# Two layers of a graph network on one core: a second dense row beside the input stage, list steps in the stage of x

## The chip, the cores and the metric

One core of a Trainium2 chip. The metric is the device time of one launch in microseconds (us), all in 32-bit floats.

## The reference

x is (8, 2048, 128), adj (2048, 2048) with about 0.4% of its entries set and a full diagonal. Two layers, each followed by a residual and a layer norm:

```python
# layer 0, on x, with R = adj
res = si[:, :, None] + sj[:, None, :] + R * w_r + g_b      # si, sj: x @ two columns of g_w
y = (res @ x) @ weight + bias
x = layernorm(x + y)
# layer 1, A1 = A2 = adj
x1 = A.T @ x ;  x2 = 2 * A.T @ x1 - x
y = relu(stack(x, x1, x2, x1, x2) @ Theta1 + bias)
x = layernorm(x + y)
```

Layer 0's sums over si, sj and g_b have rank 9 over the batch, so what remains of it is one product of the sparse R with x @ weight. Layer 1 is two products with the transposed adj ("hops").

## The kernel before, in words

The 2048 nodes are 16 blocks of 128. `Y` holds x @ weight for all 16 blocks on chip (each block 128 x 1024, 8 batches by 128). Rows 0 to 3 of R's blocks are kept transposed and dense in `at4`; their products with Y are whole ("dense rows", `full_rows`). For the rows of blocks 4 to 15, the kernel finds out which rows of each strip of columns have entries, makes lists of them, and multiplies only gathered rows.

Every instruction is tied to program order on its engine (`Tied`, line 67), so the order written is the order run on each queue. All lines are therefore recorded at L72, and groups are read by their tiles.

Stages, in order:

- **Stage of R** (loop over `R_ORDER`, line 328). Step k loads a row of blocks of adj into one of three buffers (`rc`), TensorE transposes its 16 blocks four at a time into a bank, and ScalarE copies them out, scaled, to `at4`, `rct` or `Y` (`row_groups`, line 244). `transposes` (line 237) takes banks in turn from `turns`: 6, 7, 4, 5. VectorE reduces row and column masks (lines 252 to 262). Some steps (`x_at`, line 189) also take a block of x: 8 transposes (`x_t`), then `y_of` (line 277) multiplies by `wx` into banks 2 and 3 by turns, and ScalarE copies to Y. There are NX = 10 such x blocks in this stage, and after each but the first one product of dense row 0 is accumulated in banks 0 and 1. Transposed rows of blocks 4 to 11 are stored to `rr_d` at once.
- **`pump`** (line 216) issues SP's loads and stores from the list `todo`, in its order: the rows of adj three ahead, the blocks of x six ahead, then stores of rows 12 to 15 ("s"), then copies of adj into `rr_d` ("c").
- **Stage of x** (line 666): the remaining six x blocks, each with one product of row 0. Between them: `ranked` at n = 11, `candidates` and the eight rounds of the first lists at n = 13 (VectorE: `max` and `match_replace`). Then Y is stored to `y0_d`.
- **Lists and dense rows** (lines 756 to 825): `lists_end(0)` gives the first indices; from then on GpSimd gathers. A **job** is the gathers of one list of one block: "T" four gathers, "H" three. `get_job` issues them, and `keep_job` has VectorE copy what landed into `rc` and `rct`; four jobs are in flight over four buffers (`st`), and those of blocks 0 to 3 use one buffer (`trp`). `next_job` is a keep and a get. Of the 32 jobs, 20 are fetched here. Around them TensorE does dense row 1 (banks 2, 3), `column_sums` (banks 4, 5, set to zero ahead of the stage of x), `make_ub`, dense rows 2 and 3, `make_u` of finished blocks (through banks 4, 5) and VectorE the rounds of the second lists (`rounds2`), `z_add` and `layernorm`. `lists_end(1)` (line 469) ends the second lists and the test `over`, which decides on a dense fallback at the end that isn't taken.
- **Loop over blocks 4 to 15** (line 828): `get_rows` gathers rows of `y0_d` into twelve buffers in Y (G, line 689), seven gathers a block; `own_rows`, `rank9`, `listed` multiply; `z_add`, `make_u`, `layernorm` follow. Eight jobs are fetched in it (blocks 4 to 7, 9, 11, 13, 15).
- **Two hops** (line 860), 16 blocks each with seven gathers a block; the first fetches the last four jobs.

Of the kernel before, what the change touches and what calls it, by code (L numbers as in the profile page):

```python
# [18 lines left out]
def kernel(  # L19
# [37 lines left out]
    W = 3 * P  # L57
    T_ORDER = list(range(6, NC)) + [4, 5]
    NP = LR + NC - LT
    R_ORDER = [0, 4, 5, 6, 1, 7, 8, 9, 2, 10, 11, 12, 3, 13, 14, 15]  # L60
    NX = 10
    X_ORDER = list(range(ND, NC)) + list(range(ND))
    X_SLOT = [0, 1, 3, 4, 2, 5]
    assert D == P and B == 8 and NC == 16
# [37 lines left out]
    def by4(t):  # L102
        return t.rearrange("p (b f) -> p b f", b=4)
# [79 lines left out]
    ats += [Y[:, n:n + 2].rearrange("p c b f -> p (c b f)") for n in X_ORDER[NX::2]]  # L183

    def at_of(c):
        t = at4[:, c] if c < ND else ats[(c - ND) % 5]
        return t.rearrange("p (j i) -> p j i", i=P)

    def x_at(k):
# [86 lines left out]

    def y_of(n, xt):
        for b in range(0, B, 2):
            py = bank[2 + b // 2 % 2][:, 0:2 * (D + 2)].rearrange("p (i f) -> p i f", i=2)
            for i in range(2):  # L280
                pe.matmul(py[:, i, :], xt[b // HB][:, (b + i) % HB, :], wx, start=True, stop=True)
            act.copy(Y[:, X_ORDER[n], b:b + 2, :], py[:, :, 0:D])
            act.copy(sraw[:, X_ORDER[n], b:b + 2, :], py[:, :, D:D + 2])
# [22 lines left out]
                )  # L306

    LAST = list(range(ND)) + list(range(8, NC)) + list(range(4, 8))
    js_first = [X_ORDER[0]] + [LAST[0]] * (ND - 1)

    def full_rows(c, accs, js):
        at = at_of(c)
# [33 lines left out]
    dve.tensor_add(th[:, 4, :], th[:, 2, :], th[:, 4, :])  # L346
    dve.tensor_sub(th[:, 2, :], th[:, 0, :], th[:, 4, :])
    dve.tensor_add(th[:, 0, :], th[:, 4, :], th[:, 4, :])
    dve.tensor_add(th[:, 1, :], th[:, 1, :], th[:, 3, :])

# [58 lines left out]
    dve.tensor_reduce(miss[:, 1:2], both, AX.XY, ALU.add)  # L409
    for b in bank[4:6]:  # L410
        dve.memset(b, 0.0)

    def encode2():
        dve.tensor_sub(NS_[:, 0:LT, :], NS_[:, 0:LT, :], et)
# [54 lines left out]
    def lists_end(part):  # L469
        b = bank[6 + part]  # L470
        if part == 0:
            lo, hi = 0, NT
            for r in range(2):
                pe.matmul(
                    b[64 * r:64 * r + 64, 0:NT], lists, ident[:, 64 * r:64 * r + 64], start=True,
                    stop=True, skip_group_check=True, tile_position=(0, 64 * r),
                )
        else:
            lo, hi = NT, NI
            for r in range(2):  # L480
# [12 lines left out]
        dve.scalar_tensor_tensor(rown, rown, float(NC), col[:, s], op0=ALU.mult, op1=ALU.add)  # L493
        dve.tensor_copy(idr[:, s], rown)
        if part:
            dve.tensor_reduce(miss[:, 2:3], has, AX.X, ALU.add)
            dve.tensor_sub(miss[:, 0:1], miss[:, 0:1], miss[:, 1:2])
            dve.tensor_sub(miss[:, 0:1], miss[:, 0:1], miss[:, 2:3])
            pe.matmul(
                b[0:1, 64:65], miss[:, 0:1], ones[:, 0:1], start=True, stop=True,  # L500
                skip_group_check=True,
            )
            dve.tensor_scalar(over, b[0:1, 64:65], 0.5, None, op0=ALU.is_gt)

    adj128 = adj.rearrange("n (c f) -> (n c) f", f=P)

# [135 lines left out]
    for k in range(4):  # L642
        x1t.append(rct[:, k * BD:(k + 1) * BD].rearrange("p (b f) -> p b f", b=B))

    def make_u(c, z, xt, u):
        for h in range(2):
            b = transposes([z[:, h * HB + i, :] for i in range(4)])
            act.copy(xt[:, h * HB:(h + 1) * HB, :], b)
        for h in range(2):
            b = by4(bank[4 + h])  # L650
# [11 lines left out]
        get_job()  # L662


    turns[:] = [6, 7]
    for n in range(NX, NC):
        xt = x_t(n)
        pump()
        y_of(n, xt)
        if n == 13:  # L670
            candidates()
            for r in range(8):
                round_of(lists, cand, r)
        full_rows(0, acc0, [X_ORDER[n - 1]])
        if n in (NX, NX + 1, 13):
            s_rows(X_ORDER[4 * max(0, n - NX - (n == 13))])
        if n == 11:
            ranked()
    s_rows(0)
    full_rows(0, acc0, [X_ORDER[NC - 1]])  # L680
    pump()
    assert not todo

# [69 lines left out]
        load_own(0, y0_d, c, Y[:, c] if c < 8 else ring[:, c % 2], c < 8)  # L753


    acc1 = acc_pair()
    full_rows(1, acc1, LAST[0:4])
    lists_end(0)
    get_job()
    get_job()  # L760
    encode2()
    get_job()
    get_job()
    for c0 in range(0, NC, 4):
        column_sums(c0)
    full_rows(1, acc1, LAST[4:5])
    split2()
    make_ub()
    load_z(ND + 1)
    candidates2()  # L770
    full_rows(1, acc1, LAST[5:8])
    next_job()
    rounds2([0])
    next_job()
    si_t(0)
    rank9(0, acc0)
    rounds2([1, 2])
    next_job()
    z_add(acc0, zs[0])
    rounds2([3, 4])  # L780
    next_job()
    rounds2([5, 6])
    next_job()
    rounds2([7])
    full_rows(1, acc1, LAST[8:])
    si_t(1)
    rank9(1, acc1)
    lists_end(1)
    z_add(acc1, zs[1])
    next_job()  # L790
    layernorm(zs[0], "0_0")

    acc2 = acc_pair()
    full_rows(2, acc2, LAST[:8])
    make_u(0, zs[0], x1t[0], u_of[0])
    next_job()
    layernorm(zs[1], "0_1")
    next_job()
    full_rows(2, acc2, LAST[8:])
    si_t(2)  # L800
    rank9(2, acc2)
    for _ in range(2):
        next_job()
    z_add(acc2, zs[2])
    make_u(1, zs[1], x1t[1], u_of[1])
    next_job()
    layernorm(zs[2], "0_2")

    acc3 = acc_pair()
    full_rows(3, acc3, LAST[:8])  # L810
    for _ in range(3):
        next_job()
    own0(ND)
    own0(ND + 1)
    full_rows(3, acc3, LAST[8:])
    for _ in range(2):
        next_job()
    get_rows(0, ND, "T", y0_d)
    get_rows(0, ND, "H", y0_d)
    get_rows(0, ND + 1, "T", y0_d)  # L820
    si_t(3)
    rank9(3, acc3)
# [5 lines left out]
    for c in range(ND, NC):  # L828
        if c > ND:
            if c > ND + 1:  # L830
                get_rows(0, c, "T", y0_d)
            get_rows(0, c, "H", y0_d)
        if c < 10:
            keep_job()
            if c < 8:
                get_job()
            else:
                keep_job()
        elif c % 2:
            keep_job()  # L840
# [12 lines left out]
        for n in [c - 2] if c < 14 else [12, 13] if c == 14 else [14]:  # L853
            make_u(n, zs[n], x1t[n], u_of[n])
        if c + 2 < NC:
            load_z(c + 2)
        layernorm(zs[c], f"0_{c}")


    def hop(i, src, order, there, between):  # L860
# [51 lines left out]
        for k, c in enumerate(order):  # L912
# [117 lines left out]
```

## Time and profile before

| | |
|---|---|
| median of 3 runs | 816.0 us (814.28 to 816.8) |
| the profiled execution | 811.46 us |
| its span | 809.7 us |
| TensorE, VectorE, ScalarE, GpSimd busy | 720.0, 394.8, 188.7, 443.3 us |

| stage, by the trace | us | TensorE busy | transfer engines busy |
|---|---|---|---|
| R | 16 to 105 | 76.3 of 89 | 1.07 |
| x | 105 to 140 | 31.4 of 35 | 1.07 |
| lists and dense rows | 140 to 260 | 111.3 of 120 | 0.66 |
| loop over blocks 4 to 15 | 260 to 428 | 152.2 of 168 | 0.93 |
| first hop | 428 to 629 | 180.9 of 201 | 0.93 |
| second hop | 629 to 810 | 163.5 of 181 | 0.89 |

In a line of the trace the first number is the start in us, the second the length, then the engine, the operation, out<-in by tiles, the shape and the count of records merged. A matmul of 32-bit floats leaves two records. In brackets stands how long the engine idled just before, and what released it. TensorE's busy time counts the pipeline's tail, so it overstates the work done.

### The profile page before, as it was taken

The page shows a single profiled execution, that of the slowest core. Times are in us where ns is not written, and L with a number is a line of the kernel's source. Part 1 is how long each engine was busy: PE and PEld are TensorE (multiplying, and loading weights), DVE is VectorE, ACT ScalarE, POOL GpSimd, SP SyncE. Part 2 cuts the span into 40 slices and gives each one's busy share as a digit, 9 for nine tenths or more (in the row PEclk, how much of TensorE's full clock was granted, in tenths as well). Part 3 has the DMA queues.
Part 4 walks back from the last instruction along what each step waited for, and adds up shares of the span by engine and source line. Part 5 has one row for each costly group of instructions (what it writes and reads, how often), then busy time and mean ns, then how long its engine had stood idle before and what let it go on. Part 6 is the DMA issues. An engine that isn't in the chain of part 4 may idle for free.

```text
span 809.7 us, 10066 instructions
## 1 busy us (share of the span) xinstructions
PE 720.0 (89%) x3554; PEld 365.2 (45%) x3554; DVE 394.8 (49%) x591; ACT 188.7 (23%) x439; POOL 443.3 (55%) x432
## 2 busy tenths in 40 slices
PE   4987989996999989897998788989999899999992
PEld 4766756442543334444354233433444345544441
DVE  5776586587342555655442000000000377777775
ACT  3775755101120223323232000000000011111111
POOL 1000000477677777767635677776664777787650
PEclk8998999997999999999899899999999999999996
DMA  7999999996343999999988799899999799999982
GB/s 264 340 349 352 342 311 309 321 414 215 105 148 92 306 341 351 382 377 342 328 302 315 245 347 369 308 372 392 351 362 345 259 353 357 371 386 374 378 300 70
DMA packets 165300, 253.91 MB, mean 314 GB/s; under 512 B 17255, under 2 KB 118020, under 8 KB 163192
## 3 DMA queue, kind: packets, MB, share of 16 engines
q0 software_dynamic: 49280, 146.52, 49.8%
q1 hardware_dynamic: 93200, 81.01, 30.9%
q10 hardware_dynamic: 22760, 25.63, 8.9%
q8 instruction: 30, 0.49, 0.3%
q14 instruction: 30, 0.25, 0.1%
HBM read 234.82 MB, written 58.72 MB: 363 GB/s over the span
## 4 chain that ended last, share of the span: by engine, by line
PE 48%; DMA 34%; issue 7%; ACT 4%; DVE 3%; POOL 2%; ACTq 0%; SPq 0%; POOLq 0%; DVEq 0%
PE bank L72 48%; DMA Y<-u_d,idx 14%; DMA Y<-y_d,idx 7%; DMA st<-rr_d,idx 4%; DMA ring<-in_x_dram 3%; DMA rd<-rr_d 2%; DMA rc<-in_adj_dram 1%; ACT Y L72 1%; DMA trp<-in_adj_dram,idr 1%; POOL Y L72 1%; DVE st L72 1%; ACT rct L72 1%; ACT trp L72 1%; POOL st L72 1%; ACT at L72 1%
## 5 line engine op out<-in xcount | busy, mean ns | idle before, releaser
L72 POOL DMA_INDIRECT Y<-y_d,idx x196 | 215.4, 1099 | 87.9 <-PE bank L72 39.0
L72 PE MATMUL bank<-Y,rc 128*32 128x512 f32 (+2 forms) x896 | 218.7, 609 | 22.2 <-DMA Y<-u_d,idx 19.8
L72 POOL DMA_INDIRECT st<-rr_d,idx x84 | 86.2, 1026 | 176.2 <-DVE rown L72 146.9
L72 POOL DMA_INDIRECT Y<-u_d,idx x112 | 110.9, 990 | 61.7 <-PE bank L72 25.8
L72 PEld LDWEIGHTS bank<-Y,rc 128*32 128x32 f32 (+2 forms) x896 | 58.9, 128 | 178.9 <-issue 89.9
L72 PE MATMUL bank<-Y,at 128*128 128x512 f32 x256 | 115.9, 603 | 0.0
L72 PE MATMUL bank<-Y,rct 128*32 128x512 f32 (+2 forms) x336 | 75.8, 643 | 9.0 <-DMA Y<-y_d,idx 9.0
L72 DVE TENSOR_REDUCE s<-sq 128x4 f32<-128x512 f32 x64 | 43.9, 686 | 64.4 <-ACT sq L72 64.4
L72 PEld LDWEIGHTS bank<-Y,at 128*128 128x128 f32 x256 | 47.8, 193 | 54.4 <-issue 54.3
L72 DVE COPY ring<-bank 128x512 f32<-128x512 f32 x10 | 6.9, 692 | 115.5 <-PE bank L72 115.5
L72 ACT ACTIVATE sq<-ring 128x512 f32<-128x512 f32 x44 | 27.7, 630 | 122.4 <-DVE ring L72 81.0
L72 PE MATMUL bank<-ring,rd 128*128 128x512 f32 x108 | 51.7, 601 | 3.2 <-DVE ring L72 2.5
L72 DVE TENSOR_REDUCE st<-rc 128x64 f32<-128x2048 f32 x16 | 36.5, 2283 | 32.3 <-DMA rc<-in_adj_dram 32.3
L72 PE MATMUL bank<-ident,rc 128*128 128x128 f32 (+2 forms) x302 | 40.1, 292 | 12.4 <-DMA rc<-in_adj_dram 12.4
L72 PE MATMUL bank<-th,at 128*128 128x128 f32 x384 | 47.6, 277 | 1.9 <-ACT at L72 1.9
L72 ACT COPY ring<-bank 128x512 f32<-128x512 f32 x34 | 19.9, 585 | 121.6 <-PE bank L72 121.6
L72 PEld LDWEIGHTS bank<-th,at 128*128 128x128 f32 x384 | 45.2, 192 | 6.7 <-ACT at L72 3.8
L72 PEld LDWEIGHTS bank<-Y,rct 128*32 128x32 f32 (+2 forms) x336 | 20.4, 133 | 56.5 <-issue 36.3
L72 PEld LDWEIGHTS bank<-ident,rc 128*128 128x128 f32 (+2 forms) x302 | 35.9, 153 | 18.4 <-issue 13.7
L72 PE MATMUL bank<-wx,trp 128*128 128x130 f32 x256 | 36.4, 285 | 8.4 <-ACT sraw L72 6.1
L72 DVE TENSOR_TENSOR ring<-bank,ring 128x512 f32<-128x512 f32 x26 | 17.5, 687 | 52.8 <-PE bank L72 46.3
L72 PE MATMUL bank<-ident,ring 128*128 128x128 f32 x232 | 32.2, 284 | 7.1 <-DMA ring<-in_x_dram 5.6
(142 smaller groups left out, 788.6 us busy)
## 6 DMA issues: line engine op xcount, KB each, us to landing
rc<-in_adj_dram SPq DMA_DIRECT2D x16, 1024.0 KB, 9.8
ring<-in_x_dram SPq DMA_DIRECT2D x25, 512.0 KB, 10.4
rr_d<-in_adj_dram SPq DMA_DIRECT2D x12, 1024.0 KB, 11.1
y_d<-Y SPq DMA_DIRECT2D x16, 512.0 KB, 10.8
rr_d<-rct SPq DMA_DIRECT2D x6, 1024.0 KB, 9.4
rr_d<-Y SPq DMA_DIRECT2D x6, 1024.0 KB, 11.7
u_d<-ring ACTq DMA_DIRECT2D x12, 512.0 KB, 7.2
ring<-y_d SPq DMA_DIRECT2D x11, 512.0 KB, 15.8
```

The lines of the kernel that those rows point to most:

```text
L72: return lambda *a, **k: tc.keep_in_program_order(f(*a, **k))
```

## The change

NX is 8 instead of 10, so two x blocks move from the stage of R to the stage of x. Rows 0 and 1 of R are loaded first, and each x block after the first is followed by a product of row 0 and one of row 1, in banks 0 to 3. To make room, `y_of` moves to banks 4 and 5, and the transposes of R have banks 6 and 7 alone. `ats` has six buffers instead of five. The list steps are called from within the stage of x; the zeroing of banks 4 and 5 moves behind the first round of the second lists. After the stage of x, the column sums and both ranks follow at once; row 2 uses banks 4 and 5, row 3 banks 2 and 3, and the first two `make_u` banks 0 and 1. The test `over` moves to `overflow`, after row 2. 16 jobs are fetched before the loop, ten in it (blocks 4 to 12 and 14) and six in the first hop.

```diff
-    R_ORDER = [0, 4, 5, 6, 1, 7, 8, 9, 2, 10, 11, 12, 3, 13, 14, 15]
-    NX = 10
+    R_ORDER = [0, 1, 4, 5, 6, 2, 7, 8, 9, 10, 3, 11, 12, 13, 14, 15]
+    NX = 8
...
-    todo += [("x", 10), ("x", 11), ("s", 12), ("s", 13), ("x", 12), ("x", 13), ("s", 14), ("s", 15)]
-    todo += [("x", 14), ("x", 15)] + [("c", c) for c in T_ORDER]
+    todo += [("x", 8), ("s", 12), ("x", 9), ("s", 13), ("x", 10), ("x", 11), ("s", 14), ("x", 12)]
+    todo += [("s", 15), ("x", 13), ("x", 14), ("x", 15)] + [("c", c) for c in T_ORDER]
...
-    turns = [6, 7, 4, 5]
+    turns = [6, 7]
...
-            py = bank[2 + b // 2 % 2][:, 0:2 * (D + 2)].rearrange("p (i f) -> p i f", i=2)
+            py = bank[4 + b // 2 % 2][:, 0:2 * (D + 2)].rearrange("p (i f) -> p i f", i=2)
...
-    acc0 = acc_pair()
+    acc0, acc1 = acc_pair(), acc_pair()
...
                 full_rows(0, acc0, [X_ORDER[m - 1]])
+                full_rows(1, acc1, [X_ORDER[m - 1]])
...
+    def lists_at(n):
+        if n == 9:
+            ranked()
+        if n == 10:
+            candidates()
+            for r in range(8):
+                round_of(lists, cand, r)
+            dve.tensor_reduce(miss[:, 1:2], both, AX.XY, ALU.add)
+            thetas()
+        if n == 13:
+            lists_end(0)
+            get_job()
+            get_job()
+            encode2()
+            get_job()
+            get_job()
+        if n == 14:
+            split2()
+        if n == 15:
+            candidates2()
+
     for n in range(NX, NC):
         xt = x_t(n)
         pump()
         y_of(n, xt)
...
+        lists_at(n)
+        for c, acc in enumerate((acc0, acc1)):
+            full_rows(c, acc, [X_ORDER[n - 1]])
...
+    rounds2([0])
+    for b in bank[4:6]:
+        dve.memset(b, 0.0)
+    next_job()
+    rounds2([1, 2])
+    next_job()
     for c0 in range(0, NC, 4):
         column_sums(c0)
...
     make_ub()
     load_z(ND + 1)
...
+    rounds2([3, 4])
     next_job()
     si_t(0)
+    si_t(1)
     rank9(0, acc0)
+    rank9(1, acc1)
+    rounds2([5, 6])
+    next_job()
+    rounds2([7])
+    lists_end(1)
     z_add(acc0, zs[0])
...
     z_add(acc1, zs[1])
     next_job()
     layernorm(zs[0], "0_0")
...
+    acc2 = bank[4:6]
+    full_rows(2, acc2, LAST[:5])
+    next_job()
+    next_job()
+    make_u(0, zs[0], x1t[0], u_of[0], 0)
     layernorm(zs[1], "0_1")
...
+    full_rows(2, acc2, LAST[5:11])
+    next_job()
+    make_u(1, zs[1], x1t[1], u_of[1], 0)
+    next_job()
+    full_rows(2, acc2, LAST[11:])
     si_t(2)
     rank9(2, acc2)
...
     z_add(acc2, zs[2])
+    overflow()
     next_job()
     layernorm(zs[2], "0_2")
...
+    acc3 = bank[2:4]
     full_rows(3, acc3, LAST[:8])
...
+    next_job()
+    next_job()
+    get_rows(0, ND, "T", y0_d)
+    get_rows(0, ND, "H", y0_d)
     own0(ND)
     own0(ND + 1)
     full_rows(3, acc3, LAST[8:])
...
+    keep_job()
+    keep_job()
     get_rows(0, ND + 1, "T", y0_d)
...
-        if c < 10:
+        if c < 15:
             keep_job()
...
-        if c > 8 and c % 2:
+        if c < 13 or c == 14:
             get_job()
...
-            if i == 1 and k % 2 and k < 10:
+            if i == 1 and (k % 2 and k < 12 or k == 12):
                 keep_job()
-                if k < 9:
+                if k < 12:
                     get_job()
```

More of the change, by code (lines that the diff above doesn't have):

```diff
@@ L185, in at_of @@
     def at_of(c):
-        t = at4[:, c] if c < ND else ats[(c - ND) % 5]
+        t = at4[:, c] if c < ND else ats[(c - ND) % len(ats)]
         return t.rearrange("p (j i) -> p j i", i=P)
@@ L308 @@
     LAST = list(range(ND)) + list(range(8, NC)) + list(range(4, 8))
-    js_first = [X_ORDER[0]] + [LAST[0]] * (ND - 1)
+    js_first = [X_ORDER[0]] * 2 + [LAST[0]] * (ND - 2)
     def full_rows(c, accs, js):
@@ L344, with thetas @@
     mask_columns(NC - 1)
[L346 to L349, printed above, removed]
+    def thetas():
+        dve.tensor_add(th[:, 4, :], th[:, 2, :], th[:, 4, :])
+        dve.tensor_sub(th[:, 2, :], th[:, 0, :], th[:, 4, :])
+        dve.tensor_add(th[:, 0, :], th[:, 4, :], th[:, 4, :])
+        dve.tensor_add(th[:, 1, :], th[:, 1, :], th[:, 3, :])
     e2 = rc[:, 4608:4608 + 2 * NP * HC].rearrange("p (q l) -> p q l", l=2 * HC)
@@ L408 @@
     dve.tensor_reduce(miss[:, 0:1], hs, AX.XY, ALU.add)
-    dve.tensor_reduce(miss[:, 1:2], both, AX.XY, ALU.add)
-    for b in bank[4:6]:
-        dve.memset(b, 0.0)
     def encode2():
@@ L498, in lists_end, with overflow @@
             dve.tensor_sub(miss[:, 0:1], miss[:, 0:1], miss[:, 2:3])
[L499 to L503, printed above, removed]
+    def overflow():
+        b = bank[turns[turn[0] % len(turns)]]
+        turn[0] += 1
+        pe.matmul(
+            b[0:1, 0:1], miss[:, 0:1], ones[:, 0:1], start=True, stop=True, skip_group_check=True,
+        )
+        dve.tensor_scalar(over, b[0:1, 0:1], 0.5, None, op0=ALU.is_gt)
     adj128 = adj.rearrange("n (c f) -> (n c) f", f=P)
@@ L643, with make_u @@
         x1t.append(rct[:, k * BD:(k + 1) * BD].rearrange("p (b f) -> p b f", b=B))
-    def make_u(c, z, xt, u):
+    def make_u(c, z, xt, u, o=4):
         for h in range(2):
@@ L649, in make_u @@
         for h in range(2):
-            b = by4(bank[4 + h])
+            b = by4(bank[o + h])
             for i in range(HB):
@@ L662, in next_job @@
         get_job()
-    turns[:] = [6, 7]
+    def lists_at(n):
[18 more added lines that the diff above has]
+            candidates2()
     for n in range(NX, NC):
@@ L669 @@
         y_of(n, xt)
[L670 to L678, printed above, removed]
+        lists_at(n)
+        for c, acc in enumerate((acc0, acc1)):
+            full_rows(c, acc, [X_ORDER[n - 1]])
+        if n % 4 == 0:
+            s_rows(X_ORDER[n - 4])
+        if n == 9:
+            s_rows(X_ORDER[0])
     s_rows(0)
-    full_rows(0, acc0, [X_ORDER[NC - 1]])
+    for c, acc in enumerate((acc0, acc1)):
+        full_rows(c, acc, [X_ORDER[NC - 1]])
     pump()
@@ L753, in own0 @@
         load_own(0, y0_d, c, Y[:, c] if c < 8 else ring[:, c % 2], c < 8)
[L756 to L763, printed above, removed]
+    rounds2([0])
[4 more added lines that the diff above has]
+    next_job()
     for c0 in range(0, NC, 4):
         column_sums(c0)
-    full_rows(1, acc1, LAST[4:5])
-    split2()
     make_ub()
     load_z(ND + 1)
[L770 to L773, printed above, removed]
+    rounds2([3, 4])
     next_job()
     si_t(0)
+    si_t(1)
     rank9(0, acc0)
[L777 to L781, printed above, removed]
+    rank9(1, acc1)
     rounds2([5, 6])
@@ L784 @@
     rounds2([7])
-    full_rows(1, acc1, LAST[8:])
-    si_t(1)
-    rank9(1, acc1)
     lists_end(1)
+    z_add(acc0, zs[0])
     z_add(acc1, zs[1])
@@ L791 @@
     layernorm(zs[0], "0_0")
-    acc2 = acc_pair()
-    full_rows(2, acc2, LAST[:8])
-    make_u(0, zs[0], x1t[0], u_of[0])
+    acc2 = bank[4:6]
+    full_rows(2, acc2, LAST[:5])
     next_job()
+    next_job()
+    make_u(0, zs[0], x1t[0], u_of[0], 0)
     layernorm(zs[1], "0_1")
+    full_rows(2, acc2, LAST[5:11])
     next_job()
-    full_rows(2, acc2, LAST[8:])
+    make_u(1, zs[1], x1t[1], u_of[1], 0)
+    next_job()
+    full_rows(2, acc2, LAST[11:])
     si_t(2)
     rank9(2, acc2)
-    for _ in range(2):
-        next_job()
     z_add(acc2, zs[2])
-    make_u(1, zs[1], x1t[1], u_of[1])
+    overflow()
     next_job()
     layernorm(zs[2], "0_2")
-    acc3 = acc_pair()
+    acc3 = bank[2:4]
     full_rows(3, acc3, LAST[:8])
-    for _ in range(3):
-        next_job()
+    next_job()
+    next_job()
+    get_rows(0, ND, "T", y0_d)
+    get_rows(0, ND, "H", y0_d)
     own0(ND)
@@ L815 @@
     full_rows(3, acc3, LAST[8:])
[L816 to L819, printed above, removed]
+    keep_job()
+    keep_job()
     get_rows(0, ND + 1, "T", y0_d)
@@ L832 @@
             get_rows(0, c, "H", y0_d)
-        if c < 10:
+        if c < 15:
             keep_job()
[L835 to L840, printed above, removed]
-        if c > 8 and c % 2:
+        if c < 13 or c == 14:
             get_job()
```

## The prediction

> **What bounds the kernel now.** I read the page's slices first, then TensorE's timeline, then GpSimd's, then the chain of waits.
>
> ```profile
> PE   4987989996999989897998788989999899999992
> ```
>
> ```profile
> POOL 1000000477677777767635677776664777787650
> DMA  7999999996343999999988799899999799999982
> ```
>
> A slice is 20.2 us. TensorE is near full nearly everywhere. The transfer engines are full up to 190 us and from 270 us on, but a third busy in between (slices 11 to 13). GpSimd, idle until 150 us, is then steadily busy. So no one engine bounds the whole; the bound changes by stage.
>
> Stage of R (16 to 105 us): two steps from TensorE's timeline (start, length, engine; in brackets its wait).
>
> ```profile
> 31.15 1.04 PE L72 MATMUL bank<-ident,rc 128*128 128x128 f32 x8
> 32.02 1.04 PE L72 MATMUL bank<-ident,ring 128*128 128x128 f32 x8
> 32.90 1.04 PE L72 MATMUL bank<-ident,rc 128*128 128x128 f32 x8
> 33.77 1.06 PE L72 MATMUL bank<-wx,trp 128*128 128x130 f32 x8
> 35.56 1.16 PE L72 MATMUL bank<-wx,trp 128*128 128x130 f32 x8 [0.73 <-ACT sraw L72]
> 36.55 1.88 PE L72 MATMUL bank<-Y,at 128*128 128x512 f32 x4
> 38.27 2.78 PE L72 MATMUL bank<-ident,rc 128*128 128x128 f32 x24
> ...
> 71.84 1.94 PE L72 MATMUL bank<-ident,rc 128*128 128x128 f32 x8 [3.66 <-DMA rc<-in_adj_dram]
> ```
>
> A step with an x block takes 38.27 - 31.15 = 7.12 us and waits for ScalarE; one product of dense rows (four records, two matmuls) takes 38.27 - 36.55 = 1.72 us. Waits for transfers are few: 10.0 us in all, with 6.1 us for ScalarE. The stage is a TensorE-ScalarE relay with transfers close behind.
>
> Stage of x (105 to 140 us): one block takes 109.98 - 104.70 = 5.28 us, 1.72 of it the product.
>
> Dense rows and lists (140 to 259 us): GpSimd issues one gather per 1.30 us from 150.38 us on, with one long stall, until the rows of block 4 (line label: y_d, the tensor gathered is y0_d).
>
> ```profile
> 150.38 1.16 POOL L72 DMA_INDIRECT st<-rr_d,idx  x1 [146.94 <-DVE rown L72]
> ...
> 217.95 1.00 POOL L72 DMA_INDIRECT st<-rr_d,idx  x1 [4.23 <-DVE rc L72]
> ...
> 259.40 1.00 POOL L72 DMA_INDIRECT Y<-y_d,idx  x1 [0.30 <-issue]
> ```
>
> TensorE, meanwhile, multiplies 27.6 us for each row of blocks, and idles 6.8 us at the end of the second lists:
>
> ```profile
> 189.90 0.46 PE L72 MATMUL bank<-ident,lists 96*64 96x48 f32 x4 [4.94 <-DVE lists L72]
> 192.21 0.19 PE L72 MATMUL bank<-ones,miss 128*1 128x1 f32 x2 [1.86 <-DVE miss L72]
> 192.33 16.18 PE L72 MATMUL bank<-Y,at 128*128 128x512 f32 x32
> ```
>
> Loop over blocks 4 to 15 (259.4 to 428.2 us): its first five blocks wait for gathers, since each needs 7 row gathers and 3 of a job: ten by 1.30 us, 13 us, against 11.85 us of TensorE.
>
> ```profile
> 264.79 7.33 PE L72 MATMUL bank<-Y,rct 128*32 128x512 f32 x22 [1.20 <-DMA Y<-y_d,idx]
> ...
> 295.89 5.44 PE L72 MATMUL bank<-Y,rct 128*64 128x512 f32 x10 [1.40 <-DMA Y<-y_d,idx]
> ...
> 312.97 1.98 PE L72 MATMUL bank<-Y,rct 128*128 128x512 f32 x4 [1.75 <-DMA Y<-y_d,idx]
> ...
> 326.65 1.98 PE L72 MATMUL bank<-Y,rct 128*128 128x512 f32 x4 [1.69 <-DMA Y<-y_d,idx]
> ```
>
> **What the Trainium skill says.** "TensorE: Matmul & The Clock Gate", Part 1: an idle window halves TensorE's clock until it has been busy again for some microseconds. The trace agrees: after the idle 3.66 us, eight transposes took 1.94 us instead of 1.04. "PSUM — Partial Sum Buffer", on bank collisions: guard PSUM by bank, so TensorE may not write a bank still being read. Agrees: the 0.73 us wait for ScalarE's eviction. "DMA: Bandwidth & Descriptors", "Issuing engines are not separate DMA queues": all queues interleave on the same 16 engines. Agrees: the engines stay full at 1.05 from 105 to 190 us whoever issues. "TensorE: Matmul & The Clock Gate", on queue depths: VectorE and ScalarE are strictly first-in first-out. Agrees: GpSimd's 4.23 us stall is a keep_job standing behind a layernorm.
>
> **The change, part by part.**
>
> 1. *R.* Products go from 9 to 14 (+5 x 1.72 = +8.6 us of TensorE), x blocks from 10 to 8 (2 x 3.5 = -7): about +1.6 us of work. But transposes now turn over two banks instead of four. Per bank: four transposes 0.44, 0.25 until ScalarE starts (104.70 to 105.39 less 0.44), eviction 0.70, 0.05 back: 1.44 us per two groups. A pair of steps (one without x, one with) has ten groups: y_of can begin at 6.7 us, takes 2.4, two products 3.44: 12.4 us, with ScalarE idle under the products. The trace doesn't show two banks: from below, TensorE's own work is 10.0 us a pair (transfers would then end R near 102); from above, 0.1 us more a group gives 13.4 and S = 117; I take 12.4, since worked the same way, before comes to 7.3 and 9.55 us for a step with x and a pair, where the trace has 7.12 and 9.44. From the arrival of the first x at 16.2 us (4.3 us into its pair), the stage lasts 8 x 12.4 - 3.4 - 4.3 = 91.5, plus 1.5 for the slow clock at its start: it ends at S = 109, against 104.7. The 10 us of transfer waits mostly go, since transfers now lead; that is in this figure. The order of the stores of 12 to 15 costs nothing: block 12's, which the first eviction of the x stage overwrites, can go some 15 us ahead; uncovered it would cost up to its 10 us of landing.
>
> 2. *x.* Eight blocks of 5.28 + 1.72 = 7.0 us, ranked 0.4, candidates 1.7, lists_end 0.3, split2 0.5, candidates2 2.2, last products 3.4: S + 64.6. VectorE's rounds run from S + 20.5 to S + 38 and the first lists end on TensorE at S + 40.6, unwaited; gathers start 1.6 us later, S + 42 = 151, against 150.4: the lists are not earlier. SP's copies stand behind x 15, which now needs the second x step: some 4 us later, hidden until 168 us, long ahead of the jobs that need them. Theta's sums and the count move behind the rounds, 1.5 us of VectorE that end at S + 39.5: free.
>
> 3. *Between.* Column sums 7.0, make_ub with its two evictions 2.8, ranks 3.7: S + 78. The second lists wait for VectorE: rounds from S + 58.5, 21 us, memset 1, four keeps 2: S + 82.5. So TensorE idles 4.5 us here too; overflow's 1.86 us wait is gone. Behind it stand z_add, a keep and a layernorm of 7.9 us on VectorE before make_u(0) at S + 95.6; the five products queued ahead of it end at S + 92 (slow clock: S + 94). Then make_u twice 6.5, 11 + 16 products 46.4, ranks and transposes 4: the loop starts at S + 152.5 to S + 155; I take S + 154 = **263**, 3.6 us later than 259.4. A whole row left this stretch, but it paid for its 27.6 us in R and x.
>
> 4. *Jobs.* 16 instead of 20 are fetched ahead of the loop: 60 gathers (12 x 4 + 4 x 3) instead of 72. A job's gather must wait until VectorE has kept the job four before it, and two keeps now stand behind z_add of row 2 (S + 124) and its layernorm (S + 132.6); so the last two jobs are issued by S + 141, and the rows T of 4, H of 4, T of 5 by S + 146, 150 and 155: 255, 259, 264. Before, the chain puts the wait of T of 4 that ends at 264.79 on the gather issued at 259.40, so they ended near 260, 264 and 270. Their destinations in Y come free as the last dense row reads them, from S + 125 on, in time. own0's loads, on SP, aren't passed by anything that they wait for. So GpSimd is 6 us ahead of before, although TensorE is 3.6 behind.
>
> 5. *Loop.* From that lead, blocks 4 to 9 (six) run at TensorE's 11.85 us, nearly unwaited (before: 13.2 us of waits and slow clock over blocks 4 to 8). But a job now goes with every block to 12, so from 10 on the pace is 13.1 us; 13 to 15 take 14.4, 15.2, 13.4. Sum by issue alone: the end at 417 against 428.2. Transfers set a floor: 56.1 MB took from 264 to 430 us; 1 MB more (four jobs of up to 0.39 MB) at the 365 GB/s of full slices is 157 us: 420. Late loads of z (6.5 and 6.9 us before) will cost again; I take **421**, -7.
>
> 6. *First hop.* Two jobs more, seven gathers, 9.1 us of issue where GpSimd idles after 550 us, under 0.5 MB: 0 to 3 us, I take **+1.5**. The second hop is unchanged.
>
> Sum: -7 + 1.5 = -5.5 on the profiled execution's 811.5 us, i.e. 806. The median of the runs shown is 816.0, 4.5 above that execution; carried over, **811**.
>
> **Rivals.**
>
> *The lead isn't usable (slower).* In the loop the transfer engines are 0.93 busy, mostly 0.97 to 1.04. If bandwidth, not issue, holds the first blocks, starting 3.6 us late is not made up, and the moved jobs add 1 MB, 3 us: 811.5 + 3.6 + 1.5 + 1.5 to 3 is 818 to 820, by the median 823 to 824. It decides if less than some 3 us of the 13.2 comes back. For it: those shares. Against: GpSimd's unbroken 1.30 us beat up to 335 us.
>
> *Half of it (no change).* The loop gains 5: 3.6 - 5 + 1.5 = 0, so 816.
>
> *R isn't slower.* If ScalarE's evictions overlap better than I work out and R ends with its transfers, 2 x 0.5 MB fewer, S is 102 to 105: everything comes 4 to 7 us earlier, 804 to 807; with the loop at its 417 as well, 802. Against: the relay fits two kinds of step within 3%.
>
> *It doesn't do what it says*: products beside x might be no overlap at all, only moved; step 3 already says so for x, and the forecast rests on GpSimd's lead.
>
> **Numbers.** Forecast (its own range 807.5 to 813.5) 0.42, R not slower 0.13, half 0.20, slower 0.25. Faster by over 0.3% (2.4 us, about what a measurement of this kernel can tell from no change) is the first two, 0.55; within 0.20; slower 0.25. Range: 802 to 824, from R not slower to the slower rival's end.
>
> **What would show it.** R's end (last product ahead of the first x-stage transposes): 107 to 111, pairs near 12.4 us. First gather near 151. TensorE waits at the second lists 3 to 6 us. First own rows of block 4 near 263; own rows of block 9 near 323 (263 + 5 x 11.85), against 335 if the loop gains nothing (before: 331.63). A z_add that waits for its x in most blocks, and gathers landing over 9 us after issue, would speak for the slower rival. Wrong altogether if the gathers start past 158.

## The result, and the profile after

| | before | after |
|---|---|---|
| median of 22 runs each | 814.78 us (810.09 to 820.93) | 811.03 us (806.31 to 818.08) |
| ratio | | 0.9955, 95% interval 0.9933 to 0.9976 |
| profiled execution (span) | 811.46 us (809.7) | 818.08 us (816.3) |

The kernel became faster by 0.45%, 3.75 us by the medians. The profile after shows by chance the longest of its 22 executions, so its end can't be set against the profile of before. A second profile of the same kernel (`after_third`, below: 809.29 us, span 807.5) lies 1.9 us under its median, the one of before 3.3 us under its own; it is used wherever ends are compared, and where both agree, the first is shown. The profiles of three experiments (`before_again`, `early_keep`, `lists_late`) show slow executions of their kernels, so no end is read from them.

The page's slices of the changed kernel:

```profile
PE   4999999997999998988798888898899999999992
```

```profile
POOL 1000000477747876776344677776774777776740
DMA  8999999999326799999969799899999799999982
```

TensorE no longer dips in slices 3, 4 and 6 (8, 7 and 8 before; R). GpSimd has a hole in slice 12, at 224 to 245 us.

TensorE's timeline in R: one pair of steps. A bank is a buffer that TensorE writes and ScalarE empties. Nearly every line of eight transposes, two groups of four, now waits for ScalarE to empty one of two banks; waits for transfers of `rc` are gone.

```profile
47.48 1.04 PE L72 MATMUL bank<-ident,rc 128*128 128x128 f32 x8
48.86 1.24 PE L72 MATMUL bank<-ident,rc 128*128 128x128 f32 x8 [0.34 <-ACT Y L72]
50.29 1.24 PE L72 MATMUL bank<-ident,rc 128*128 128x128 f32 x8 [0.20 <-ACT Y L72]
51.73 1.24 PE L72 MATMUL bank<-ident,ring 128*128 128x128 f32 x8 [0.20 <-ACT Y L72]
53.12 1.24 PE L72 MATMUL bank<-ident,rc 128*128 128x128 f32 x8 [0.15 <-ACT trp L72]
54.19 1.06 PE L72 MATMUL bank<-wx,trp 128*128 128x130 f32 x8
55.45 1.16 PE L72 MATMUL bank<-wx,trp 128*128 128x130 f32 x8 [0.21 <-ACT sraw L72]
56.45 3.60 PE L72 MATMUL bank<-Y,at 128*128 128x512 f32 x8
59.88 1.04 PE L72 MATMUL bank<-ident,rc 128*128 128x128 f32 x8
```

The pair takes 59.88 - 47.48 = 12.40 us, and two groups 1.43 us (48.86 to 50.29; 1.44 foreseen). Under the pair's two products of dense rows (3.43 us, from 44.05 and from 56.45 on) ScalarE soon has nothing to empty, and idles until the next pair's first transposes:

```profile
48.12 1.27 ACT L72 ACTIVATE Y<-bank,wr 128x512 f32<-128x512 f32 x2 [3.43 <-PE bank L72]
```

So as the change is built, the products stand in this relay with nearly their full length. R ends at 109.51, and the first gather follows 42.2 us later (before: 45.7). TensorE at the second lists and at the first `make_u`, then GpSimd's first gather:

```profile
191.20 0.46 PE L72 MATMUL bank<-ident,lists 96*64 96x48 f32 x4 [3.46 <-DVE lists L72]
...
204.06 1.09 PE L72 MATMUL bank<-ident,ring 128*128 128x128 f32 x8 [1.87 <-DVE ring L72]
```

```profile
151.69 1.16 POOL L72 DMA_INDIRECT st<-rr_d,idx  x1 [148.25 <-DVE rown L72]
```

By stage (us; own rows of a block mark its start; loop = blocks 4 to 15):

| | R ends | loop starts | blocks 4 to 8 | 9 to 12 | 13 to 15 | loop ends | first hop | rest |
|---|---|---|---|---|---|---|---|---|
| before | 104.7 | 259.4 | 72.2 | 51.7 | 44.9 | 428.2 | 193.6 | 187.9 |
| after, first | 109.5 | 262.1 | 66.5 | 57.4 | 48.3 | 434.3 | 192.7 | 189.4 |
| `after_third` | 109.3 | 261.9 | 66.3 | 54.8 | 41.7 | 424.7 | 194.3 | 188.5 |

Before against `after_third`: +2.5 up to the loop, -5.9 in it, +0.7 and +0.6 behind it; with less rounding that makes -2.2, the difference of the spans. The two executions after agree within 0.5 us up to block 9, so the 5.7 to 5.9 us that blocks 4 to 8 gain show in both; what follows differs by more than the whole gain. What makes the first slow lies there, mostly one late load for own rows of block 14 with a slow clock after it (blocks 13 and 14 take 6.6 us more than in `after_third`):

```profile
402.08 2.49 PE L72 MATMUL bank<-ring,rd 128*128 128x512 f32 x4 [4.07 <-DMA rd<-rr_d]
```

SP issues a block's two loads, its own rows (`ring`) and then its block of R (`rd`), when TensorE is done with the own rows of the block two before it. For block 14, first here, then in `after_third`:

```profile
372.12 10.37 SPq L72 DMA_DIRECT2D ring<-y_d  x1
382.54 1.18 SPq L72 DMA_DIRECT2D rd<-rr_d  x1
```

```profile
371.36 3.43 SPq L72 DMA_DIRECT2D ring<-y_d  x1
374.85 1.33 SPq L72 DMA_DIRECT2D rd<-rr_d  x1
```

The issue of the first load alone held SP for 10.37 us instead of 3.43 (0.32 in `after_third` at 344.06), so `rd` went out 7.7 us later, and TensorE could start only 19.5 us after that. Why an issue is held so long, these traces don't show.

The waits of TensorE from loop start to loop end (who waited for whom, total us, times, longest), before, then `after_third`:

```profile
PE bank L72 <- DMA Y<-y_d,idx: 9.0, 6, 1.7
PE bank L72 <- DVE ring L72: 2.5, 1, 2.5
...
PE bank L72 <- DMA rd<-rr_d: 0.6, 1, 0.6
```

```profile
PE bank L72 <- DMA Y<-y_d,idx: 7.3, 9, 1.8
PE bank L72 <- ACT at L72: 1.4, 6, 0.2
```

So the waits for gathered rows hardly shrank in sum over the loop (in blocks 4 to 8 from 7.5 to 3.7 us); they came later, none cost the clock (TensorE was granted 1.00 of its full clock over the loop, 0.96 before), and the wait of own rows was absent in this execution. The 2.5 us before stand at own rows of block 13, 20.3 us after SP's issue of their `rd`, so that they are probably such a late load as well, though the profile names VectorE.

### The profile page after: what moved, and what is told of

It reads as the page before. It is cut to its first block, busy times and chain, and to the rows that moved or that the text cites. A ratio compares the mean times of both kernels' runs of the same rounds, so it can differ in the third digit from the quotient of the medians.

```text
span 816.3 us, 10067 instructions
## 1 busy us (share of the span) xinstructions
PE 732.8 (90%) x3554; PEld 364.9 (45%) x3554; DVE 394.7 (48%) x591; ACT 192.7 (24%) x439; POOL 445.2 (55%) x432
## 4 chain that ended last, share of the span: by engine, by line
PE 52%; DMA 29%; issue 6%; ACT 6%; DVE 3%; POOL 2%; ACTq 0%; POOLq 0%; SPq 0%; DVEq 0%
PE bank L72 52%; DMA Y<-u_d,idx 12%; DMA Y<-y_d,idx 8%; DMA st<-rr_d,idx 2%; DMA rd<-rr_d 2%; ACT Y L72 2%; DMA ring<-in_x_dram 2%; POOL Y L72 1%; ACT rct L72 1%; ACT trp L72 1%; DMA trp<-in_adj_dram,idr 1%; DVE s L72 1%; DVE ring L72 1%; ACT at L72 1%; DVE st L72 1%
## 5 line engine op out<-in xcount | busy, mean ns | idle before, releaser
L72 POOL DMA_INDIRECT Y<-y_d,idx x196 | 212.0, 1081 | 93.2 <-PE bank L72 38.0
L72 POOL DMA_INDIRECT st<-rr_d,idx x84 | 90.3, 1075 | 183.5 <-DVE rown L72 148.3
L72 PE MATMUL bank<-ident,rc 128*128 128x128 f32 (+2 forms) x302 | 45.0, 297 | 12.6 <-DMA rc<-in_adj_dram 6.6
L72 PEld LDWEIGHTS bank<-ident,rc 128*128 128x128 f32 (+2 forms) x302 | 33.8, 150 | 25.5 <-issue 9.1
## 6 DMA issues: line engine op xcount, KB each, us to landing
rr_d<-in_adj_dram SPq DMA_DIRECT2D x12, 1024.0 KB, 10.8
```

The lines of the kernel that those rows point to most:

```text
L72: return lambda *a, **k: tc.keep_in_program_order(f(*a, **k))
```

## The experiments

There are four groups of experiments. In two of them, and in the result above, the kernel before took 815 us; in two others 869 us, one of these on the very chip that gave 815 us in the next. Ratios are to the kernel before in the same group.

### The yardsticks

`after_third` is the changed kernel, beside `jobs20` and `no_gathers`:

> The changed kernel without an edit, beside the next three on one chip, as their yardstick. My theory: R ends at 108.5 to 110 and the first gather is at 150.5 to 152, as in both executions so far, and the ratio to the kernel before is 0.990 to 0.997. Rival (the gain hangs on the chip): a ratio outside that.

Measured: 811.15 us, ratio 0.9956 (0.9925 to 0.9987), R's end 109.27, first gather 151.44: as expected. Two further yardsticks are from the first group at 869 us.

> The changed kernel once more, without an edit, for a second profiled execution. My theory: in the first one, the late part of the loop over blocks (402 to 434 us) and the slow clock after waits were larger than is usual, so that here the loop takes 166 to 170 us instead of 172.1, the span lies near 811, and R ends at 109 and the loop starts at 262 to 263 as before. Rival (the change itself makes the late part of the loop slower): the loop takes 172 us again.

Measured: ratio 0.9901 (0.9861 to 0.9940), R's end 108.70 with the pair at 12.40 us again, but the loop started at 277.2 and took 174.1, span 846.0. The theory failed in its numbers from the lists on, as the whole group was slower.

> The kernel before once more, without an edit, for a second profiled execution; the loop over blocks took 168.8 us in the first. My theory: 168 to 172 us here, R ends at 104 to 105, the loop starts at 259 to 260, and blocks 4 to 8 take 70 to 73 us. Rival (one execution can't be compared with another at all): R's end or the loop's start differ by over 2 us between the two executions.

Measured: ratio 1.0057 (1.0031 to 1.0084) to itself, which tells how far a ratio of this group can be trusted: some 0.6%. R ended at 107.83 and the loop started at 283.2: the rival held. For the loop's start and all behind it the trace shows where the time went, to waits of TensorE for which it names no release (`issue`), but not why:

```profile
314.99 3.78 PE L72 MATMUL bank<-th,at 128*128 128x128 f32 x16 [15.29 <-issue]
```

So stage times are compared below only within a group, R's end across groups where all its values are given, and times after 150 us, where these standstills occur, only in the groups at 815 us.

### Four banks in R

```diff
-    turns = [6, 7]
+    turns = [6, 7, 4, 5]
...
-            py = bank[4 + b // 2 % 2][:, 0:2 * (D + 2)].rearrange("p (i f) -> p i f", i=2)
+            yb = turns[turn[0] % 4] if shared[0] else 4 + b // 2 % 2
+            turn[0] += shared[0]
+            py = bank[yb][:, 0:2 * (D + 2)].rearrange("p (i f) -> p i f", i=2)
```

(`shared` ends with R, and `turns` is 6, 7 from then on. The changed kernel has these four banks in R as well, but two are kept for transposes and two for products with the weight; here both kinds take turns on all four.)

> The changed kernel with the transposes and the products with the weight in R turning over four banks (6, 7, 4, 5) instead of two and two. My theory (two banks make R a relay between TensorE and ScalarE): a pair of steps falls from 12.4 us to 10.0 to 10.6, R ends at 100 to 103 instead of 109.5, now held by transfers, and all of what follows comes 6 to 8 us earlier: the ratio to the changed kernel is 0.990 to 0.993. Rival 1 (R is bound by TensorE's added products and not by banks): a pair stays at 12 us, no change. Rival 2 (the earlier end of R is lost again, because transfers or the lists hold what follows): R ends at 101 but the loop starts at 261 or later, and the total is within 0.2% of the changed kernel.

Measured: ratio 0.9817 (0.9767 to 0.9866) beside 0.9901 of the changed kernel. R ends at 104.62 instead of 108.70, the first gather is at 146.80 instead of 150.89. Steps now wait for transfers:

```profile
62.12 3.60 PE L72 MATMUL bank<-Y,at 128*128 128x512 f32 x8
65.56 1.91 PE L72 MATMUL bank<-ident,rc 128*128 128x128 f32 x16
71.20 1.11 PE L72 MATMUL bank<-ident,rc 128*128 128x128 f32 x8 [3.73 <-DMA rc<-in_adj_dram]
73.32 1.94 PE L72 MATMUL bank<-ident,ring 128*128 128x128 f32 x8 [1.01 <-DMA ring<-in_x_dram]
```

A pair took 10.4 to 11.5 us, one with a long wait for transfers 17.5. The eight executions with two and two banks in all these groups ended R at 108.7 to 110.9 us, the three with four by turns at 104.6, 106.0 and 106.6. The split of the banks, not TensorE's added work, cost R its 3 to 4 us, so the theory holds and rival 1 falls. R ended 1.6 us later than the 103 expected at most; the total fell by 0.8%, the size expected, and little more than the 0.6% to which this group can be trusted.

### Row 1 out of R

```diff
-    turns = [6, 7]
+    turns = [6, 7, 2, 3]
...
-                full_rows(1, acc1, [X_ORDER[m - 1]])
...
+    full_rows(1, acc1, X_ORDER[:NX - 1])
```

> The changed kernel with the second dense product taken out of R: the seven products of row 1 that R had are made after R in one piece, and R's transposes turn over four banks (6, 7, 2, 3). My theory (the product beside x in R is paid for nearly in full, since R is a relay close to TensorE's own work): R ends at 98 to 102 instead of 109.5, the seven products then take 12 us, and the stage of x starts at 110 to 114; the total is 0 to 4 us above the changed kernel. Rival (products beside x in R lie beside transfers and evictions and cost nothing): R ends at 105 to 109, the stage of x starts 8 to 12 us later, and the total rises by 8 to 12 us.

Measured: ratio 0.9913 (0.9884 to 0.9942), 0.1% above the changed kernel, which the group can't tell from nothing. The trace speaks more clearly. R's last product with the weight is followed by one of row 0 and the seven of row 1:

```profile
102.13 13.90 PE L72 MATMUL bank<-Y,at 128*128 128x512 f32 x32
115.87 1.04 PE L72 MATMUL bank<-ident,ring 128*128 128x128 f32 x8
```

One product takes 1.72, so R itself ends at 102.13 + 1.72 = 103.9, against 104.6 to 106.6 with four banks by turns and row 1 inside. So with enough banks seven products (12 us of TensorE) cost R 0.8 to 2.8 us. Without them R waited 13.9 us for transfers and its mean granted clock was 0.89; with them (`four_banks`) it was 9.6 us and 0.96. My theory, that they are paid nearly in full, falls for this R; the rival is right on that, though the stage of x starts 7.2 us later than in the changed kernel, not 8 to 12. This run has two banks more for R than `four_banks`, and it doesn't test R as the change has it, with two and two banks, where the products stand in the relay.

### The lists where they were

```diff
-        if n == 9:
+        if n == 11:
             ranked()
-        if n == 10:
+        if n == 13:
             candidates()
...
-        if n == 13:
-            lists_end(0)
...
-            candidates2()
...
+    lists_end(0)
+    get_job()
+    get_job()
...
+    encode2()
+    get_job()
+    get_job()
+    for c0 in range(0, NC, 4):
+        column_sums(c0)
+    split2()
+    candidates2()
     rounds2([0])
```

> The changed kernel with the steps of the lists where the kernel before has them, counted from the stage's end: ranks at x 11, candidates at x 13, the first lists' end, the first jobs, the encoding, the column sums, the splitting and the second candidates after the stage of x, in front of the second rounds. My theory (moving them up only makes good for the x stage's two further blocks and added product): the first gather is at 172 to 176 us instead of 151.5, the second lists end some 15 to 22 us later, the loop starts 10 to 18 us later and the total is 8 to 15 us above the changed kernel. Rival (the jobs' fetches have slack until the loop, so the order of the lists is of no weight): 0 to 3 us above.

Measured in the second group at 869 us: ratio 0.9997 (0.9962 to 1.0033), 0.96% above the 0.9901 of `after_again` in the first, some 8 us. The first gather, and TensorE at the second lists:

```profile
172.81 1.16 POOL L72 DMA_INDIRECT st<-rr_d,idx  x1 [169.37 <-DVE rown L72]
```

```profile
226.17 0.45 PE L72 MATMUL bank<-ident,lists 96*64 96x48 f32 x4 [12.93 <-DVE lists L72]
```

The theory holds. Without the lists moved up, the change gains nothing: moving them makes no gather earlier than before, but otherwise the first comes 21 to 22 us later.

### The jobs as before

```diff
-    next_job()
-    next_job()
-    get_rows(0, ND, "T", y0_d)
-    get_rows(0, ND, "H", y0_d)
+    for _ in range(3):
+        next_job()
     own0(ND)
...
-    keep_job()
-    keep_job()
+    for _ in range(3):
+        next_job()
+    get_rows(0, ND, "T", y0_d)
+    get_rows(0, ND, "H", y0_d)
```

(In the loop and the first hop, gets and keeps stand as in the kernel before.)

> The changed kernel with the jobs spread as in the kernel before: 20 fetched ahead of the loop over blocks instead of 16, none beside blocks 8, 10, 12 and 14, two fewer in the first hop. My theory (GpSimd's 1.30 us a gather sets the pace, so that the spread only moves the time): GpSimd is 6 to 8 us later when the loop starts, blocks 4 to 8 take 4 to 8 us longer, blocks 9 to 12 take 4 to 6 us less, and the total is within 3 us of the changed kernel. Rival (the lead on GpSimd is the whole gain): the total is 5 us or more above the changed kernel, that is no better than the kernel before.

Measured: 822.66 us, ratio 1.0101 (1.0043 to 1.0158), 11.5 us above `after_third`, slower than before. Blocks 4 to 8 took 78.8 us, 9 to 12 51.3, 13 to 15 48.8. GpSimd's last job gather ahead of the loop and its first row of H of block 4, and TensorE's wait for that:

```profile
269.05 0.99 POOL L72 DMA_INDIRECT st<-rr_d,idx  x1 [0.30 <-issue]
270.35 1.74 POOL L72 DMA_INDIRECT Y<-y_d,idx  x1 [0.30 <-issue]
```

```profile
275.27 7.44 PE L72 MATMUL bank<-Y,rct 128*64 128x512 f32 x12 [7.70 <-DMA Y<-y_d,idx]
```

The theory, that the spread only moves time, falls, and the rival holds: blocks 9 to 12 gave back 3.5 us, blocks 4 to 8 lost 12.5, and the late blocks lost 7.1 more, with a 3.39 us wait for `rd` and a slow clock. Four jobs fewer ahead of block 4 are worth more than the whole gain of the change; without them its other parts are a loss of 1%. Whether the kernel before would gain as much by this spread of jobs alone wasn't tried.

### Gathers left out, and gathers made small

```diff
+        if 16 <= got[0] - 1 < 24:
+            return
```

> The changed kernel without the gathers of jobs 16 to 23, which it fetches beside blocks 4 to 11; their blocks of lists then work on what the buffers held before, so the output isn't the reference's. My theory (GpSimd and transfers hold the loop at 13.1 us a block): the loop falls from 172 to some 160 to 165 us, and the total by 6 to 12 us. Rival (TensorE with its slow clock and late loads of z hold the loop): the loop falls by under 3 us.

Measured: 801.63 us, ratio 0.9865 (0.9806 to 0.9924), 9.5 us below `after_third`. The loop took 156.7 us, 6.1 less than in `after_third`: blocks 4 to 8 59.0, which is TensorE's own 5 x 11.8, blocks 9 to 12 57.0, 13 to 15 40.7. No wait for gathered rows is left in it, and yet blocks 9 to 12 didn't get faster, with waits of 0.84 and 3.89 us at own rows and a slow clock (0.91 over these blocks):

```profile
350.89 3.75 PE L72 MATMUL bank<-ring,rd 128*128 128x512 f32 x4 [3.89 <-DVE ring L72]
```

The profile names VectorE, but the load of this block's `rd` had been issued only 19.2 us before, behind an issue of 7.57 us. The same order shows in the other executions with such a wait at 815 us: SP was held 5.8 to 10.4 us by the issue of own rows, and TensorE started 19.0 to 20.9 us after the issue of `rd`. So the job gathers hold blocks 4 to 8, and from 9 on these loads are late as well.

```diff
-                gather(
-                    s[:, n * 2 * P:(n + 1) * 2 * P], rr_d[c - ND].rearrange("n m f -> n (m f)"), idx,
-                    i, N,
-                )
+                gather(
+                    s[:, n * 2 * P:n * 2 * P + 32],
+                    rr_d[c - ND].rearrange("n m (k f) -> (n m k) f", f=32), idx, i, N,
+                )
```

(For jobs 16 to 23 only.)

> The changed kernel with the gathers of jobs 16 to 23 cut to 32 of the 256 columns of each row: as many instructions on GpSimd, an eighth of the bytes; the rest of these tiles is what the buffers held before, so the output isn't the reference's. The kernel without these gathers was 9.5 us below the changed one. If GpSimd's issue sets the pace of the loop: within 2.5 us of the changed kernel. If the bytes do: within 2.5 us of the kernel without these gathers, that is 7 us or more below the changed kernel. In between: both.

Measured in the second group at 869 us: ratio 0.9784 (0.9718 to 0.9851), 1.2% below the 0.9901 of the first, about as far as without the gathers. That speaks for the bytes; but in its trace the loop took 173.2 us, in that of `after_again` 174.1, and the intervals are as wide as the question. It is not settled.

### The keeps ahead of row 2's addition

In the changed kernel GpSimd stands still before the loop (`after_third`):

```profile
224.71 1.00 POOL L72 DMA_INDIRECT st<-rr_d,idx  x1 [0.30 <-issue]
234.49 1.00 POOL L72 DMA_INDIRECT st<-rr_d,idx  x1 [8.78 <-DVE rc L72]
```

Its next job waits for a keep, the keep stands behind `z_add` of row 2 on VectorE, and that waits 17.25 us for TensorE.

```diff
+    for _ in range(3):
+        next_job()
     si_t(2)
     rank9(2, acc2)
     z_add(acc2, zs[2])
     overflow()
-    next_job()
     layernorm(zs[2], "0_2")
...
-    next_job()
-    next_job()
     get_rows(0, ND, "T", y0_d)
```

> The changed kernel with three keeps of jobs (each with the next fetch) moved ahead of the addition and the layernorm of row 2, so that VectorE does them in the 17 us in which it waits for that row, and GpSimd's next fetch doesn't stand 8.8 us behind them. My theory (GpSimd's lead sets the first blocks, and this standstill is what the lead lacked): the gap of 8.8 us at 225 to 234 us falls under 3 us, the waits for gathered rows in blocks 5 to 10 (6 us and more) mostly go, the loop over blocks takes 155 to 160 us instead of 162.8, and the total is 4 to 8 us below the changed kernel, ratio to the kernel before 0.986 to 0.991. Rival 1 (bytes hold the loop): GpSimd is ahead, but the waits stay and the total falls by under 2 us. Rival 2 (VectorE then waits for a job's rows in front of the addition): the fourth dense row's start slips and the loop starts 2 us or more later.

Measured in the second group at 869 us: ratio 0.9894 (0.9832 to 0.9956), against the 0.9901 of the first no difference that can be told. In the trace GpSimd still stands 6.26 us for a keep up to 216.8 us, but no longer than 2.4 us from there to the rows, and blocks 5 to 7 take 11.8 us each. But row 2's end waited 8.39 us for ScalarE, which itself stood twice for what the trace doesn't show (`remote`):

```profile
249.40 0.59 ACT L72 COPY ring<-bank 128x512 f32<-128x512 f32 x1 [7.89 <-remote]
257.90 0.59 ACT L72 COPY ring<-bank 128x512 f32<-128x512 f32 x1 [7.91 <-remote]
```

Inconclusive on the time.

### Early keeps and four banks together

> The kernel with the early keeps and with transposes and the products with the weight in R turning over four banks, both together. My theory: the two gains lie in different stages and add: R ends 4 us earlier (at 104 to 105 instead of 109), the loop starts 4 us earlier, and the total is 4 to 7 us below that with the early keeps alone, 8 to 14 below the changed kernel, ratio to the kernel before 0.979 to 0.986. Rival (transfers hold the loop, so that an earlier start is waited away): no better than the early keeps alone by more than 2 us.

The two edits above. Measured in the same group: ratio 0.985 (0.9781 to 0.9919), 0.4% below the early keeps alone; the intervals overlap. The same kernel in the second group at 815 us:

> The kernel with the early keeps and four banks once more, for the case that it gets a chip on which the kernel before takes some 815 us; there the changed kernel had ratios of 0.9955 and 0.9956. My theory (both gains are real, and the standstills of 3 to 10 us in which ScalarE and TensorE waited for nothing that the trace shows hid them where the kernel before takes 869 us): R ends at 104 to 105, GpSimd has no gap over 3 us between 200 us and its first rows of block 4, the loop starts at 257 to 259 and takes 155 to 161 us, and the ratio is 0.982 to 0.989. Rival (transfers hold the loop at its end whatever starts earlier): the loop ends at 422 us or later and the ratio is 0.993 or more.

Measured: **802.87 us**, ratio **0.9844** (0.9799 to 0.9889), 8.3 us below `after_third`, faster than both kernels. R ends at 106.0, GpSimd has no gap of 1 us or more from 200 us to 257.9, where it waits 4.34 us for TensorE to free a buffer, the loop starts at 257.0, and blocks 4, 5 and 6 run at TensorE's rate. From TensorE's timeline:

```profile
257.01 1.88 PE L72 MATMUL bank<-Y,rd 128*128 128x512 f32 x4
...
268.82 1.88 PE L72 MATMUL bank<-Y,rd 128*128 128x512 f32 x4
...
280.62 1.88 PE L72 MATMUL bank<-Y,rd 128*128 128x512 f32 x4
...
292.43 1.88 PE L72 MATMUL bank<-Y,rd 128*128 128x512 f32 x4
```

Blocks 4 to 8 took 61.4 us instead of 66.3. But blocks 9 to 12 took 57.7 and 13 to 15 45.6 (one wait for `rd`, 2.15 us), so that the loop took 164.8 us and not 155 to 161, and ends at 421.8, only 2.9 us before that of `after_third`. Both theories were half right: the ratio is the first's, but of the 9.8 us won by block 9 (4.9 at the start, 4.9 in blocks 4 to 8) 6.8 are given back from block 9 on, as the rival has it. Another 3.3 us came in the first hop (191.0 against 194.3); why, these runs don't show. Nor do they show the share of each edit in the 8.3 us, since each alone was measured only at 869 us.

## Why the prediction was right, point by point

Predicted: 811, -5 from the 816.0 shown; measured 811.03, -3.75 from a kernel before that over 22 runs has 814.78. So the agreement is in part luck: the median carried over was 1.2 us too high, the sum of -5.5 some 2 us too large, and the two errors cancel.

1. **R** held: pairs of 12.40 us (12.4 foreseen), end at 109.5, 108.7 and 109.3 (109), transfer waits gone. The relay over two banks was priced right, with ScalarE idle under the products. What it left out: with all four banks by turns the products would be nearly free (0.8 to 2.8 us for 12).
2. **x** held: 7.0 us a block, first gather at 151.7 (151).
3. **Between** held: TensorE idles 3.46 us at the second lists (4.5) and 1.20 for ScalarE's `sit` (not foreseen); the loop starts at 262.1 and 261.9 (263).
4. **Jobs** held nearly: rows T of 4, H of 4 and T of 5 were issued by 245, 257 and 262 us (255, 259, 264). T of 4 came earlier because GpSimd issued it at 239.55 us ahead of two jobs (six gathers) that the program has before it: the sentence in the section on the kernel, that the order written is the order run, isn't true of GpSimd's queue. What changed the order isn't shown. The 9 us standstill behind row 2's addition was worked out here, but taken as harmless.
5. **Loop**: the direction held, the term was mis-sized. Foreseen were blocks 4 to 9 "at TensorE's 11.85 us, nearly unwaited", 59.2 for the first five; they took 66.5 and 66.3, so that own rows of block 9 came at 328.6 and 328.2, halfway between the 323 foreseen and the 335 of no gain: a lead of 6 us is used up as soon as a job goes with each block. Without the standstill (and with four banks) they took 61.4, without the job gathers 59.0. For the whole loop 158 were foreseen, 10.8 less than before; `after_third` has 162.8, the first execution 172.1. The late load of own rows came in the first execution (4.07 us), in `early_four_again`, `jobs20` and `no_gathers`, and not in `after_third`; by blocks 9 to 15 of the two executions after it costs up to 9 us, much of the spread of one kernel.
6. **First hop**: +1.5 foreseen, -0.9 and +0.7 measured.

Of the rivals, *the lead isn't usable* is refuted: 5.9 us came back in blocks 4 to 8, above its point of 3. Of its signs, a z_add waits for its x in two blocks of the first execution and in one of `after_third`, in two before; the gathers of rows landed 9.4 us after issue, just over its 9, but 9.0 before. *R isn't slower* is false for two and two banks and came nearly true with four by turns: R ended at 104.6 to 106.6 (its 102 to 105), and with the early keeps as well it gave 802.9 us, within its 802 to 807. *Half of it* asked for a gain of 5 in the loop; `after_third` has 5.9, nearer to that than to the forecast's 10.8. The total came nearer to the forecast because the loop started 2.5 us later instead of 3.6 and the median fell 1.6 us more than the span. *It doesn't do what it says* holds for R as the change has it, where the products stand in the relay; `four_banks` and `row1_late` show that this is due to the banks and not to the products.

What stays open: whether GpSimd's issue or the bytes set blocks 9 to 12, why SP's issue of own rows is held for up to 10 us in most executions and not in all, and what the third dense product's banks are worth. That part wasn't tried alone; by the first trace its five products, at 191.58 to 202.2, end 1.9 us before `make_u` of row 0 could start; in banks 0 and 1 they would wait for the addition of row 0 (the two rows' additions start at 193.38 and take 2.48, so until some 194.6) and end 1 us after it. So 1 us is an estimate of it, from these starts.

## What to carry to other kernels

Before adding work beside a relay between two engines, count the banks that each kind of step can turn over: with four banks shared by turns the work was nearly free here, with the same four split two and two R took 3 to 4 us more. A queue's lead is made by what is left out ahead of the first consumer, and lost by one standstill: look for the wait of an idle engine that holds a step another queue needs, and move the step ahead of the wait. And take two profiles of one kernel before explaining a difference of 1% between two executions.

## What was not expected of the hardware

- The same two kernels took 815 and 869 us in different groups, on one chip even. In the groups at 869 us TensorE stands for up to 15 us at a time (15.29 us above) and ScalarE for up to 37 with waits labelled issue or remote, and TensorE's all come after GpSimd has begun to gather (150 us on); at 815 us neither has one over 0.1 us. The cause isn't in these traces.
- A gather of GpSimd isn't always 1.00 us: in `after_third` nine of those up to 330 us took 1.7 to 2.0 (1.90 at 235.79). What the gathers took over 1.00 us sums to 8.4 us there and to 4.8 before; the difference is over half of a lead of 6 us.
- R over two banks, which no transfer holds, ended at 108.7 to 110.9 in the groups at 869 us and at 109.3 to 110.4 at 815; R of the kernel before, which waits for transfers, at 107.8 and 104.7.
